# Attention weights made in layer 1, weight loads on GpSimd's queue, and the first two diffusions made among the projections of layer 2

## The chip, the cores and the metric

The kernel runs on one core of one Trainium2 chip. The metric is device time in microseconds (us) of one execution, lower is better. Times are medians of several executions; a profile is one further execution with the hardware profiler on.

## The reference, cut to what matters

Four graph layers run one after another on 4096 nodes with 256 features each, every one followed by a residual sum and a layernorm. Layer 0 is a masked attention over the adjacency matrix, layer 1 a dense product with it, layer 2 two steps of graph diffusion and top-p attention, layer 3 a mean over neighbours. The change lies in layer 1's first instructions and in layer 2:

```python
def layer1(x, adj, weight, bias):
    support = x @ weight
    return (diagonal(adj) + adj) @ support + bias

def layer2(X, S, W1, W2, W3, U1, U2, ln_g, ln_b):
    R = S + eye(N); R = R / R.sum(-1)
    Z, Xf, Xa = 0, X, X
    for n in range(2):
        q = Xa @ W1.T @ W2.T            # attention weights W1, W2, W3
        k = Xa @ W3.T
        probs = softmax(q @ k.T)
        A = top_p(probs, 0.9)           # keep the nucleus of each row, renormalise
        Xf = R @ Xf                     # diffusion
        Xa = A @ Xa                     # attention
        Z = Z + Xf @ U1[n].T + Xa @ U2[n].T   # projections
    h = X + Z
    return layernorm(h) * ln_g + ln_b

x = layernorm(x + layer1(x, adj, ...))
x = layernorm(x + layer2(x, adj, ...))
```

## The kernel before, in words

Rows are handled in 32 blocks of 128. X (the features, float32, all 32 blocks) and XD (a product's right-hand side, split into a high and a low part so that one 512-wide matmul does both) stay on the chip.

**Who decides the order.** Outside the parts under `manual_schedule` the framework orders each engine's instructions by its own estimate of when each is ready, so an instruction may stand far from its place in the source. On the chip each engine takes its own list strictly in order. A DMA is issued by an engine's queue (SP, ACT or POOL) at its place in that engine's list; if it must wait (for a buffer's last reader, say), everything behind it on that engine waits too.

**Layer 1.** `layer1` first transposes X in groups of four blocks (L108, copies L109), multiplies with w1 (L743) and splits the result into XD (L126, L127). Then, block by block, it multiplies the adjacency with XD (L764, 32 matmuls of 512 columns to a block), adds, normalises (L769 to L96) and writes the block to memory (L773, POOL's queue). Tiles `xT1[0]` and `xT1[1]` take the transposes in turn.

**Layer 2, its start.** `weights(0)` loads U1 and U2 of step 0 into `wt` (two DMAs, L1512) and ln_b into `affine` (L1513), on ACT's queue. Before that, in the source, W1, W3 and W2 are loaded into part of `es[0]` (L802, L803, ACT's queue too), W1 is transposed (L806, copied by L807), multiplied with W2 (L810), and the product and W3 are copied into `wkq` (L811, L812).

**keys.** For each of 8 groups of four blocks: transpose X (L891), copy to SBUF (L892; in step 0 the transposes of blocks 16 to 31 stay in `es[1]`), multiply with `wkq` (L896), copy keys and queries (L898, L899, L901, L902), transpose the keys (L905, L907), write the queries to memory (L910); moments of the keys (L913). Then the moments are worked into a small matrix (L914 to L932), and the centred keys go to `kT` (L924, L925, L926).

**scores, spreads, nucleus.** `scores(b)` multiplies a block's queries with all keys (L968) and takes the exponential (L970) into `es[b % 3]`. `spreads` makes a width for each row (L941, L945 to L955). `guessed` estimates a cut from it on ACT (L977, L1021), with a full pass on DVE for the first two blocks (L1055). `nucleus` finds the exact cut on DVE (L1122, L1126, small operations) and masks the row (L1176).

**project.** `project(step, b)` multiplies two blocks with `wt` (four L1453). In step 0, for blocks under 16, X is transposed anew (L1444, copied by L1447); for 16 and over `es[1]` is read. ACT writes XD's high part (L1457) and the part for Z (L1458, sent to memory by L1460), DVE the low part (L1459); POOL adds `affine` to X (L1462) and writes that (L1463). In step 1 ACT writes X and a summand (L1466, L1468) and POOL adds it to what was loaded (L1465, L1469, L1470). The loop takes the pairs b + 16 modulo 32 in the order b = 0, 2, ... 30. So `scores(1)`, which overwrites `es[1]`, stands after the eighth pair.

**Then** `weights(1)` loads `wt` and `affine` for step 1, `diffusion` multiplies blocks 0 and 1 of the adjacency with XD (L179; the pieces, four 128x128 tiles each, are loaded by SP, L176, three buffers), `diffused` and `keep` finish them (L1377, L1379, L1380, L1389), and the hand-ordered loop over blocks starts. In it each block has eight parts: four transposes of the masked row (L1325, copied by L1327) and four matmuls with X (L1334), with scores and the diffusion of a later block between them.

In step 1 the last such loads are of layer 3's weights (`w3` into `wt`, L1572, ACT's queue).

Of the kernel before, what the change touches and what calls it, by code (L numbers as in the profile page):

```python
# [9 lines left out]
F32 = mybir.dt.float32  # L10
# [13 lines left out]
P = 128  # L24
# [26 lines left out]
def row_broadcast(v, n):  # L51

    return bass.AP(tensor=v.tensor, offset=v.offset, ap=[[0, P], [1, n]])


class Net:
# [76 lines left out]
    def open_split(self):  # L133

        pool = self.ctx.enter_context(self.tc.tile_pool(name="split", bufs=1))
        self.XD = pool.tile([P, self.NB, 2, self.D], F32R, name="XD")

    def out_space(self):

# [583 lines left out]
        self.xT1 = [pool.tile([P, 2, 4 * P], F32, name=f"xT{i}") for i in range(2)]  # L723

    def add_w1(self):
        pool = self.pool1
        self.weight1, self.bias1 = self.load_w(pool, self.w1, "w1"), self.load_row(pool, self.b1, "bias1")

    def layer1(self):
        nc, tc, NB, D, X = self.nc, self.tc, self.NB, self.D, self.X  # L730
        with self.ctx1 as ctx:
            pool, w1, bias, dg = self.pool1, self.weight1, self.bias1, self.diagr
            work = ctx.enter_context(tc.tile_pool(name="l1w", bufs=2))
            psum = ctx.enter_context(tc.tile_pool(name="l1ps", bufs=2, space=PSUM))
            XD = self.XD
            for g in range(NB // 4):
                xT = self.transposed(psum, work, X[:, 4 * g:4 * g + 4, :], "xT", out=self.xT1[g % 2])
                if 1 <= g <= 4:
                    self.layernorm(work, self.later[g - 1], self.later[g - 1])
                for q in range(4):  # L740
                    ps = psum.tile([P, 512], F32, name="ps_sup")
                    for c in range(2):
                        nc.tensor.matmul(ps[:, :D], xT[:, c, q * P:(q + 1) * P], w1[:, c, :],  # L743
                                         start=(c == 0), stop=(c == 1))
                    self.split(XD[:, 4 * g + q], ps[:, :D])
            pd = psum.tile([P, 512], F32, name="ps_sup")
            for jc in range(NB):
                nc.tensor.matmul(pd, dg[:, jc:jc + 1].to_broadcast([P, P]), XD[:, jc].rearrange("p s d -> p (s d)"),
                                 start=(jc == 0), stop=(jc == NB - 1))
            row = pool.tile([P, D], F32, name="row1")  # L750
            nc.vector.tensor_add(row, pd[:, :D], bias)
            nc.vector.tensor_add(row, row, pd[:, D:])

            nas = []
            ahead = self.adj_pieces(work, nas, 0)
            for b in range(NB):
                ps = psum.tile([P, 512], F32, name="ps_adj")
                now, ahead = ahead, None
                for g, a in enumerate(now):

                    self.keep(work, a, b, g)
                    for k in range(8):
                        jc = g * 8 + k
                        nc.tensor.matmul(ps, a[:, k, :], XD[:, jc].rearrange("p s d -> p (s d)"),  # L764
                                         start=(jc == 0), stop=(jc == NB - 1))
                if b + 1 < NB:
                    ahead = self.adj_pieces(work, nas, b + 1)
                xb = X[:, b:b + 1, :]
                nc.vector.tensor_add(xb[:, 0], xb[:, 0], ps[:, :D])  # L769
                nc.vector.tensor_add(xb[:, 0], xb[:, 0], ps[:, D:])  # L770
                nc.vector.tensor_add(xb[:, 0], xb[:, 0], row)
                self.layernorm(work, xb, xb)
                nc.gpsimd.dma_start(self.xd[b, :, 0, :], xb[:, 0])  # L773


    def layer2(self):
        nc, tc, NB, D, X, N = self.nc, self.tc, self.NB, self.D, self.X, self.N
        A = 64
        HALF = N // 2
        with ExitStack() as ctx:  # L780
            self.ctx3 = ExitStack()
            rows2 = self.ctx3.enter_context(tc.tile_pool(name="l2", bufs=1))
            pool = ctx.enter_context(tc.tile_pool(name="l2s", bufs=1, side="right"))
            work = ctx.enter_context(tc.tile_pool(name="l2w", bufs=2, side="right"))
            psum = self.psum2 = self.ctx3.enter_context(tc.tile_pool(name="l2ps", bufs=2, space=PSUM))
# [5 lines left out]


            wt = pool.tile([P, 2, 2, D], F32, name="wt")
            wkq = pool.tile([P, 2, 2, A], F32, name="wkq")

            es = [rows2.tile([P, 4096], F32, name=f"e{i}") for i in range(3)]
            pre = es[0]
            aw1, aw3 = (pre[:, i * 128:(i + 1) * 128].rearrange("p (c m) -> p c m", c=2) for i in range(2))
            aw2 = pre[:A, 256:256 + A]
            w1 = pre[:A, 320:576].rearrange("p (c m) -> p c m", c=2)  # L800
            for t, w in ((aw1, self.aw1t), (aw3, self.aw3t)):
                nc.scalar.dma_start(t, w.rearrange("(c p) m -> p c m", p=P))  # L802
            nc.scalar.dma_start(aw2, self.aw2t)  # L803
            for c in range(2):
                pt = psum.tile([P, 512], F32, name="ps_tp")
                nc.tensor.transpose(pt[:A, :P], aw1[:, c, :], self.ident)  # L806
                nc.scalar.copy(w1[:, c, :], pt[:A, :P])  # L807
            for c in range(2):
                pt = psum.tile([P, 512], F32, name="ps_tp")
                nc.tensor.matmul(pt[:, :A], w1[:, c, :], aw2, start=True, stop=True)  # L810
                nc.vector.tensor_copy(wkq[:, c, 1, :], pt[:, :A])  # L811
                nc.vector.tensor_copy(wkq[:, c, 0, :], aw3[:, c, :])  # L812
            affine = pool.tile([P, D], F32, name="affine")
            rdeg = pool.tile([P, NB], F32, name="rdeg")
            nc.vector.tensor_scalar_add(rdeg, self.deg, 1.0)
# [41 lines left out]
            XD = self.XD  # L857
# [9 lines left out]
            def keys(step, src):  # L867
# [50 lines left out]
                nc.tensor.matmul(pc[:, :2 * A + 1], id2.rearrange("p s m -> p (s m)"), mom1, start=True, stop=True)  # L918
                nc.vector.tensor_copy(mom, pc[:, :2 * A + 1])

                for c in range(N // 1024):
                    cols = slice(c * 1024, (c + 1) * 1024)
                    kc = qs[:A, cols]
                    nc.vector.tensor_scalar(kc, kc, mom[:A, 2 * A:], None, op0=ALU.subtract)  # L924
                    nc.scalar.copy(kT[:A, cols], kc)  # L925
                    nc.vector.tensor_sub(kT[A:, cols], kc, kT[:A, cols].bitcast(F32))  # L926
# [418 lines left out]
            def diffusion(step, b):  # L1345


                pr = ps1.tile([P, 512], F32, name="ps_r")
                yield from self.adj_product(work, pr, b, lambda jc: XD[:, jc])
                return pr  # L1350
# [56 lines left out]
            def whole(steps):  # L1407

                while True:
                    try:  # L1410
                        next(steps)
                    except StopIteration as end:
                        return end.value
# [94 lines left out]
            def weights(step):  # L1508

                ut = (self.u1t, self.u2t)[step]  # L1510
                for i in range(2):
                    nc.scalar.dma_start(wt[:, :, i], ut[1 - i].rearrange("(c p) m -> p c m", p=P))  # L1512
                nc.scalar.dma_start(affine, row_broadcast((self.ln_b, self.ln_g)[step], D))  # L1513

            def piece(step, b, g, a=None):

# [8 lines left out]
            def times(ps, a, g, first=False, ks=range(4)):  # L1525

                for k in ks:
                    jc = 4 * g + k
                    nc.tensor.matmul(ps, a[:, k, :], XD[:, jc].rearrange("p s d -> p (s d)"),  # L1529
                                     start=(first and k == 0), stop=(jc == NB - 1))  # L1530

            def early(step, todo, banks, made):

# [12 lines left out]
            for step in range(2):  # L1546
# [8 lines left out]
                if step == 1:  # L1555
                    whole(scores(1, queries(1)))
                    guess = drained(guessed(step, 1))

                for b in range(0, NB, 2):
                    if b == 16 and step == 0:  # L1560
                        whole(scores(1, queries(1)))
                        guess = drained(guessed(step, 1))
                    if edge:
                        v = result(edge)
                        if v is not None:
                            rs[0], edge = v, None
                    project(step, (b + 16) % NB)
                if step == 0:
                    weights(1)
                else:  # L1570
                    for k in range(2):
                        nc.scalar.dma_start(wt[:, :, k], self.w3[k * D:(k + 1) * D].rearrange("(c p) m -> p c m", p=P))  # L1572

                if step == 0:
                    xb = base(step, 0)
                    pr = whole(diffusion(step, 0))
                    whole(diffused(step, 0, pr, xb))
                    whole(keep(step, 0, xb))
                    pr = whole(diffusion(step, 1))
                aTs = [turn(es[0], g) for g in range(2)]  # L1580
                q = queries(2)
                if step == 0:
# [350 lines left out]
```

## Time and profile before

| | us |
|---|---|
| median of 3 executions | 4052.07 |
| lowest, highest | 4050.99, 4052.44 |
| the profiled execution, its own time | 4052.79 |
| its span in the trace | 4051.1 |

The 1.7 us between the profiled execution's time and its span lie around the traced instructions. PE is the matmul engine, PEld its weight loads, DVE the vector engine, ACT the scalar engine, POOL GpSimd, SP the engine that only issues DMAs. A line of the timeline gives the start in us, the duration, engine, source line, operation, written and read tile, shapes, and the count; in brackets the engine's idle time ahead of it and what ended it. In the windows each engine's busy time is followed by its number of instructions, then come the granted TensorE clock (1.00 is full), the DMA engines' busy share, and GB/s.

### The profile page before, as it was taken

How to read it: one execution, taken by the hardware profiler on the slowest of the kernel's cores; microseconds unless marked ns; L12 is line 12 of the kernel's file. 1: busy time of each engine (PE TensorE's matmuls, PEld its weight loads, DVE VectorE, ACT ScalarE, POOL GpSimd, SP SyncE). 2: the span in 40 equal slices, each digit the busy share in tenths (PEclk: the TensorE clock that was granted, in tenths of full speed). 3: DMA queues.
4: the chain of work that ended last, by engine and by line, in shares of the span. 5: the costliest groups of instructions: out<-in, count | busy, mean ns of one | idle time of the engine just before them, and what ended most of it. 6: DMA issues, size and time to landing. Idle time of an engine off the chain costs nothing. (4 is left out here: it accounts for less than half of the span.)

```text
span 4051.1 us, 68763 instructions
## 1 busy us (share of the span) xinstructions
PE 3914.2 (97%) x25081; PEld 3388.4 (84%) x25081; DVE 2994.8 (74%) x6643; ACT 2755.4 (68%) x5127; POOL 1076.8 (27%) x1322
## 2 busy tenths in 40 slices
PE   8999999999999999799999999999999999999899
PEld 7899999999999788468888888864888888888687
DVE  7643228999999444548787887847899999999364
ACT  5543339999998322358888888835888888888132
POOL 0111110111333122301111111113455555555211
PEclk9999999999999999899999999999999999999999
DMA  4765547334221596433233323363333333335541
GB/s 137 230 208 177 179 151 214 96 103 125 70 87 51 222 379 270 121 107 97 95 99 98 103 92 102 105 227 98 105 116 106 103 113 111 103 114 189 185 159 47
DMA packets 322442, 556.42 MB, mean 137 GB/s; under 512 B 72134, under 2 KB 148550, under 8 KB 317990
## 3 DMA queue, kind: packets, MB, share of 16 engines
q1 hardware_dynamic: 239920, 395.13, 30.1%
q0 software_dynamic: 27664, 84.44, 6.2%
q10 hardware_dynamic: 54502, 72.27, 5.2%
q8 instruction: 203, 3.33, 0.3%
q14 instruction: 153, 1.25, 0.1%
HBM read 385.78 MB, written 165.94 MB: 136 GB/s over the span
## 5 line engine op out<-in xcount | busy, mean ns | idle before, releaser
L1334 PE MATMUL ps_a<-X,aT 128*128 128x256 f32 x4096 | 970.5, 380 | 1.3 <-ACT h L1475 1.1
L1334 PEld LDWEIGHTS ps_a<-X,aT 128*128 128x128 f32 x4096 | 776.0, 190 | 125.5 <-issue 3.3
L319 PE MATMUL acc<-gm,gt 128*128 128x198 bf16 x8192 | 706.4, 249 | 23.0 <-DMA gm<-gmd 6.7
L319 PEld LDWEIGHTS <-gt 128*128 128x128 fp8e4 x8192 | 703.1, 98 | 26.3 <-issue 9.3
L266 ACT ACTIVATE sg<-lpb,nlc 128x1024 fp8e4<-128x1024 f32 x636 | 667.2, 1135 | 61.3 <-DVE gt L268 38.6
L179 PE MATMUL ps_r<-XD,adj_piece 128*128 128x512 f32 x1952 | 548.1, 416 | 5.3 <-DMA adj_piece<-adjs 5.2
L537 PE MATMUL pz<-src,ar 128*128 128x264 f32 x4096 | 511.3, 288 | 14.2 <-DVE ar L527 12.2
L537 PEld LDWEIGHTS pz<-src,ar 128*128 128x128 f32 x4096 | 507.7, 190 | 17.7 <-DVE ar L527 11.8
L1061 ACT ACTIVATE ja<-e,nc 128x2048 uint8<-128x2048 f32 x240 | 480.9, 2004 | 2.0
L1327 ACT COPY aT<-ps_tp 128x512 f32<-128x512 f32 x512 | 295.9, 578 | 228.3 <-PE ps_tp L1325 226.4
L179 PEld LDWEIGHTS ps_r<-XD,adj_piece 128*128 128x128 f32 x1952 | 346.1, 190 | 78.9 <-issue 13.4
L530 ACT ACTIVATE nb<-a 128x512 uint8<-128x512 f32 x256 | 156.5, 630 | 288.6 <-DMA a<-in_adjt_dram 279.7
L1126 DVE MAX8 cand<-v 128x8 f32<-128x256 f32 x1024 | 347.1, 411 | 4.4
L1176 DVE SCALAR_TENSOR_TENSOR e<-e,edge 128x512 f32<-128x512 f32 x512 | 347.2, 750 | 2.2
L1325 PE MATMUL ps_tp<-ident,e 128*128 128x128 f32 x2048 | 308.2, 273 | 0.0
L1122 DVE SCALAR_TENSOR_TENSOR v<-e,hi 128x2048 f32<-128x2048 f32 x128 | 301.4, 2355 | 2.4
L1325 PEld LDWEIGHTS ps_tp<-ident,e 128*128 128x128 f32 x2048 | 257.1, 142 | 50.9 <-issue 0.5
L968 PE MATMUL ps_logit<-kT,q 128*128 128x512 f32 x1024 | 278.0, 414 | 12.1 <-DVE kT L926 6.6
L260 DVE TENSOR_SCALAR sg<-lpb,nlc 128x1024 fp8e4<-128x1024 f32 x384 | 285.1, 778 | 5.9 <-DVEq L357 3.9
L970 ACT ACTIVATE e<-ps_logit 128x1024 f32<-128x1024 f32 x256 | 259.8, 1025 | 29.9 <-PE ps_logit L968 28.8
L527 DVE CAST ar<-a 128x1024 fp32r<-128x1024 f32 x128 | 88.6, 693 | 232.9 <-PE pz L537 231.9
L764 PE MATMUL ps_adj<-XD,adj_piece 128*128 128x512 f32 x1024 | 243.5, 398 | 0.0
(383 smaller groups left out, 5497.0 us busy)
## 6 DMA issues: line engine op xcount, KB each, us to landing
adj_piece<-adjs SPq DMA_DIRECT2D x552, 256.0 KB
a<-in_adjt_dram SPq DMA_DIRECT2D x256, 256.0 KB
adjs<-adj_piece SPq DMA_DIRECT2D x96, 512.0 KB
na<-nad SPq DMA_DIRECT2D x64, 512.0 KB
nad<-nb POOLq DMA_DIRECT2D x128, 128.0 KB, 3.4
lpb<-lpd POOLq DMA_DIRECT2D x32, 512.0 KB, 4.0
na<-nad ACTq DMA_DIRECT2D x16, 1024.0 KB
gmd<-gb ACTq DMA_DIRECT2D x64, 198.0 KB
```

The costliest lines, as they stand in the source:

```text
L179: nc.tensor.matmul(ps, a[:, k, :], rhs(jc).rearrange("p s d -> p (s d)"), start=(jc == 0), stop=(jc == self.NB - 1))
L260: nc.vector.tensor_scalar(sg[:, k, :], lpb, nlc[:, 4 * g + k, h:h + 1], 2.0 ** -5, op0=ALU.is_ge, op1=ALU.mult, saturate=False)
L266: nc.scalar.activation(sg[:, k, :], lpb, AF.Sign, scale=-1.0, bias=nlc[:, 4 * g + k, h:h + 1], saturate=False)
L319: nc.tensor.matmul(acc[:, q, :6 * C1], gt[:, k, q * P:(q + 1) * P], gm0[:, k, :] if head0 else gm[:, jc, hh, :], start=(jc == 0 and q % 2 ...
L537: nc.tensor.matmul(pz[q][:, t, :W], ar[:, q, k, :], src[:, jc, t, s], start=(jc == 0 and s == 0), stop=(jc == NB - 1 and s == 1))
L1061: nc.scalar.activation(ja, e[:, s * HALF:(s + 1) * HALF], f, bias=nc1, accum_out=fs[:, i + s:i + s + 1])
L1122: nc.vector.scalar_tensor_tensor(v, ec, hi, ec, op0=ALU.is_lt, op1=ALU.mult, accum_out=sb[:, s:s + 1])
L1126: nc.vector.max(cand[:, 8 * j:8 * j + 8], v[:, k * 256:(k + 1) * 256])
L1176: nc.vector.scalar_tensor_tensor(ec, ec, edge[:, j:j + 1], ec, op0=ALU.is_ge, op1=ALU.mult)
L1325: nc.tensor.transpose(pt[:, k * P:(k + 1) * P], e[:, jc * P:(jc + 1) * P], self.ident)
L1327: nc.scalar.copy(aT, pt)
L1334: nc.tensor.matmul(pa[:, :D], aT[:, k * P:(k + 1) * P], X[:, jc, :], start=(jc == 0), stop=(jc == NB - 1))
```

## The change

1. The attention weights are loaded in layer 0, on POOL's queue, into `xT1[1]`, and `wkq` is made at the start of `layer1`. `wkq` moves to a pool that outlives layer 1.
2. The loads of `wt` and `affine` go from ACT's queue to POOL's: in step 0 before the keys, after the projections, and layer 3's weights after step 1's projections.
3. `project(step, 16)` is made inside `keys`, before the centred keys, in both steps; the loop skips it.
4. In step 0 the diffusions of blocks 0 and 1 are no longer made after the projections: from the pair b = 16 on, each turn of the loop adds four matmuls of each (`partly`), with the pieces in the order 4, 5, 6, 7, 0, 1, 2, 3. They have the PSUM tiles ps_a and ps_r.

```diff
+        self.wkq = pool.tile([P, 2, 2, 64], F32, name="wkq")      # open_split
...
     def add_w1(self):
         self.weight1, self.bias1 = ...
+        aw1, aw3, aw2, _ = self.attention_parts()
+        for t, w in ((aw1, self.aw1t), (aw3, self.aw3t)):
+            nc.gpsimd.dma_start(t, w.rearrange("(c p) m -> p c m", p=P))
+        nc.gpsimd.dma_start(aw2, self.aw2t)
+
+    def attention_parts(self):
+        A, t = 64, self.xT1[1]
+        halves = [t[:, 0, i * P:(i + 1) * P].rearrange("p (c m) -> p c m", c=2) for i in range(2)]
+        return [*halves, t[:A, 0, 2 * P:2 * P + A], t[:A, 1, :2 * P].rearrange("p (c m) -> p c m", c=2)]
+
+    def attention_weights(self, psum):
+        nc, A = self.nc, 64
+        aw1, aw3, aw2, w1 = self.attention_parts()
+        for c in range(2):
+            pt = psum.tile([P, 512], F32, name="ps_sup")
+            nc.tensor.transpose(pt[:A, :P], aw1[:, c, :], self.ident)
+            nc.scalar.copy(w1[:, c, :], pt[:A, :P])
+        for c in range(2):
+            pt = psum.tile([P, 512], F32, name="ps_sup")
+            nc.tensor.matmul(pt[:, :A], w1[:, c, :], aw2, start=True, stop=True)
+            nc.vector.tensor_copy(self.wkq[:, c, 1, :], pt[:, :A])
+            nc.vector.tensor_copy(self.wkq[:, c, 0, :], aw3[:, c, :])
...
             XD = self.XD
+            self.attention_weights(psum)                          # layer1
             for g in range(NB // 4):
...
-            (the same loads, on ACT's queue, transposes, matmuls and copies in layer2, in es[0] and ps_tp)
...
+                project(step, 16)                                 # keys, after the moments
                 for c in range(N // 1024):
...
                 for i in range(2):                                # weights
-                    nc.scalar.dma_start(wt[:, :, i], ut[1 - i].rearrange("(c p) m -> p c m", p=P))
-                nc.scalar.dma_start(affine, row_broadcast((self.ln_b, self.ln_g)[step], D))
+                    nc.gpsimd.dma_start(wt[:, :, i], ut[1 - i].rearrange("(c p) m -> p c m", p=P))
+                nc.gpsimd.dma_start(affine, row_broadcast((self.ln_b, self.ln_g)[step], D))
...
+            def partly(ps, b, g):
+                a = piece(0, b, g)
+                for k in range(4):
+                    nc.tensor.matmul(ps, a[:, k, :], XD[:, 4 * g + k].rearrange("p s d -> p (s d)"),
+                                     start=(g == 4 and k == 0), stop=(g == 3 and k == 3))
...
+                if step == 0:
+                    firsts = [ps1.tile([P, 512], F32, name=name) for name in ("ps_a", "ps_r")]
                 for b in range(0, NB, 2):
...
-                    project(step, (b + 16) % NB)
+                    if b:
+                        project(step, (b + 16) % NB)
+                    if b >= 16 and step == 0:
+                        for row in range(2):
+                            partly(firsts[row], row, (b // 2 - 4) % 8)
                 if step == 0:
                     weights(1)
                 else:
                     for k in range(2):
-                        nc.scalar.dma_start(wt[:, :, k], self.w3[...])
+                        nc.gpsimd.dma_start(wt[:, :, k], self.w3[...])
                 if step == 0:
                     xb = base(step, 0)
-                    pr = whole(diffusion(step, 0))
-                    whole(diffused(step, 0, pr, xb))
+                    whole(diffused(step, 0, firsts[0], xb))
                     whole(keep(step, 0, xb))
-                    pr = whole(diffusion(step, 1))
+                    pr = firsts[1]
```

In the changed program the framework's lists differ only near these places. PE has the same number of matmuls as before. The new lines get their names here: L745 to L752 make the attention weights, L1523 and L1524 are `weights`' loads, L1547 is `partly`'s matmul; all other lines are named by their number before the change.

More of the change, by code (lines that the diff above doesn't have):

```diff
@@ L725, in add_w1 @@
     def add_w1(self):
-        pool = self.pool1
+        nc, pool = self.nc, self.pool1
         self.weight1, self.bias1 = self.load_w(pool, self.w1, "w1"), self.load_row(pool, self.b1, "bias1")
+        aw1, aw3, aw2, _ = self.attention_parts()
[18 more added lines that the diff above has]
+            nc.vector.tensor_copy(self.wkq[:, c, 0, :], aw3[:, c, :])
     def layer1(self):
@@ L793, in layer2 @@
             wt = pool.tile([P, 2, 2, D], F32, name="wt")
-            wkq = pool.tile([P, 2, 2, A], F32, name="wkq")
+            wkq = self.wkq
             es = [rows2.tile([P, 4096], F32, name=f"e{i}") for i in range(3)]
[L797 to L812, printed above, removed]
             affine = pool.tile([P, D], F32, name="affine")
@@ L1571, in layer2 @@
                     for k in range(2):
-                        nc.scalar.dma_start(wt[:, :, k], self.w3[k * D:(k + 1) * D].rearrange("(c p) m -> p c m", p=P))
+                        nc.gpsimd.dma_start(wt[:, :, k], self.w3[k * D:(k + 1) * D].rearrange("(c p) m -> p c m", p=P))
                 if step == 0:
                     xb = base(step, 0)
-                    pr = whole(diffusion(step, 0))
-                    whole(diffused(step, 0, pr, xb))
+                    whole(diffused(step, 0, firsts[0], xb))
                     whole(keep(step, 0, xb))
-                    pr = whole(diffusion(step, 1))
+                    pr = firsts[1]
                 aTs = [turn(es[0], g) for g in range(2)]
```

## The prediction

> **What bounds the kernel now.** I read the page's busy times first:
>
> ```profile
> PE 3914.2 (97%) x25081; PEld 3388.4 (84%) x25081; DVE 2994.8 (74%) x6643; ACT 2755.4 (68%) x5127; POOL 1076.8 (27%) x1322
> ```
>
> PE is busy 97% of the span. A block loop behind the change has no gap (80.00 of 80 us from 1820 to 1900), so time won on PE ahead of that loop should stay won. So I looked for idle PE where the diff works, in windows from the end of layer 1 to the first loop:
>
> ```profile
> core 0: us, PE busy (x) PEld busy (x) DVE busy (x) ACT busy (x) POOL busy (x), PEclk, DMA share, GB/s
> 1620.00:1632.00 12.00, 5.44 (x28) 4.32 (x29) 3.95 (x33) 2.39 (x4) 3.21 (x5) 0.79 0.48 145
> 1632.00:1669.00 37.00, 29.58 (x177) 18.46 (x175) 19.60 (x33) 17.41 (x25) 14.63 (x15) 0.92 0.69 176
> 1669.00:1695.00 26.00, 25.82 (x109) 16.70 (x110) 14.19 (x26) 11.75 (x34) 12.77 (x14) 0.89 0.20 79
> 1695.00:1706.00 11.00, 1.06 (x9) 0.82 (x7) 4.33 (x1) 4.66 (x16) 3.70 (x4) 0.66 0.23 86
> 1706.00:1764.00 58.00, 54.74 (x149) 26.48 (x148) 35.19 (x81) 25.67 (x63) 0.60 (x2) 0.98 0.18 63
> 1764.00:1792.00 28.00, 22.60 (x88) 16.52 (x86) 2.52 (x5) 4.39 (x10) 1.09 (x2) 0.88 0.56 185
> ```
>
> Length minus PE busy, added up, is 32.8 us of idle PE in 172 us, and the clock is below 1.00 after each pause. PE's waits name the pauses:
>
> ```profile
> PE ps_tp L1444 <- ACT aT L1447: 11.4, 2, 9.9
> PE ps_tp L806 <- DMA adj_piece<-adjs: 4.8, 1, 4.8
> PE ps_r L179 <- DMA adj_piece<-adjs: 3.9, 4, 1.8
> PE ps_logit L968 <- DVE kT L926: 3.6, 1, 3.6
> ```
>
> The longest is no slow copy. ACT's timeline shows what it stood behind:
>
> ```profile
> 1690.61 0.39 ACT L977 ACTIVATE z<-z,cs,t 128x1 f32<-128x1 f32 x1 [0.16 <-ACT z L977]
> 1700.14 0.35 ACTq L1513 DMA_DIRECT2D affine<-in_ln_g_dram  x1
> 1700.59 0.39 ACT L977 ACTIVATE z<-z,qsp,t 128x1 f32<-128x1 f32 x1 [9.59 <-POOL part L1462]
> ```
>
> The load of step 1's `affine` sits early in ACT's list and may not overwrite what POOL still adds. POOL makes one pair's add every 4.1 us and begins the last at 1698.86. So ACT stood 9.59 us; behind it stood the estimate (L977, L1021) that DVE's pass L1055 needs, and the copy L1447 that PE needs. At the other pause, layer 2's start, ACT's first copy L892 stands behind five weight loads. Those of L802 and L803 wait for layer 1's memory. The PE timeline shows where that leads:
>
> ```profile
> 1627.71 0.61 PE L806 MATMUL ps_tp<-ident,e 128*64 128x128 f32 x2 [4.82 <-DMA adj_piece<-adjs]
> ...
> 1631.25 3.13 PE L896 MATMUL ps_tp<-e,wkq 128*128 128x512 f32 x4
> ...
> 1705.50 1.11 PE L1444 MATMUL ps_tp<-ident,X 128*128 128x128 f32 x4 [9.94 <-ACT aT L1447]
> 1706.83 18.42 PE L1453 MATMUL ps_logit<-wt,e 128*128 128x512 f32 x40 [0.21 <-DVE XD L1459]
> ...
> 1771.49 3.78 PE L179 MATMUL ps_r<-XD,adj_piece 128*128 128x512 f32 x8 [1.83 <-DMA adj_piece<-adjs]
> ```
>
> **What the Trainium skill says.** "DMA: Bandwidth & Descriptors", in the anatomy of one DMA on the gpsimd path: the DMA engines wait on no semaphore; the issuing engine's sequencer does, before dispatch. ACT's 9.59 us agree. The same page, on issuing engines not being separate DMA queues: all share 16 engines, so moving a load wins only the issuer's time and waits. The windows cannot test that. "TensorE: Matmul & The Clock Gate", Part 1: half clock after an idle window of some 3.4 us. The trace agrees in kind, and at shorter gaps too: after 1.83 us idle, eight L179 took 3.78 us, later ones 2.14. "SBUF — State Buffer", on DVE blocking DMA: DVE can hold up GpSimd's writing of descriptors. No row here tests it; it is what could make POOL's loads dearer than their 0.72 to 0.78 us (L1463).
>
> **The change, part by part.** I replayed the changed lists with the durations of before.
>
> (1) Attention weights in layer 1. Ahead of L743 stand 2 transposes, 2 ACT copies, 2 matmuls and 4 small DVE copies: 0.6 + 0.5 + 0.6 us of PE and copies (L806, L807, L810), partly beside L108, whose transposes ran 1.06 us and whose tile copies follow. L743 begins at about 1331.05 for 1329.76: **+1.3 us** (0 if the wait for DVE's L325 covers it; +3 if DVE, where 0.85 us of copies stand in front, delays the tiles). The three loads in layer 0 cost nothing: POOL there is some 10% busy and the data is needed far later.
>
> (2) Layer 2's start. L806 to L812 and ACT's five issues go. POOL now issues `wt` (2 x 0.75 us) about where the last block's normalisation runs there, so L96 ends at 1624.15 for 1623.36. ACT's first L892 then runs 1624.2 to 1625.2, and L896 begins at 1625.25 for 1631.25: **-6.0 us** (-6.6 without POOL's delay; -3.5 if it still stands until the transfer that ended L806's wait, 1627.7).
>
> (3) A projection beside the keys. A group of keys takes 3.79 us, paced by L896, L898, L899/L901 in turn; PE is idle about 0.9 us in it. Eight L1453 records at 0.44 us (20 in 8.85), 3.5 us, go into that, and the list puts the first `partly` matmuls there too. I take +0.8 to the moments' end: L918 begins at about 1658.5 for 1663.74 (**-5.2 so far**), with 3.5 us of later work done (0 to +3.5 on the delay).
>
> (4) The `affine` load stands on POOL behind the adds that it waits for. Behind it on POOL are the guesses of the first nucleus (L1143, L1157), not needed before about 1710, and the adds end near 1699.5: no cost. ACT runs on; L1055 can begin near 1686.7 for 1701.67. The projections that went on at 1706.83 go on at 1692.1: **-14.7 so far**, with 8 of the 64 `partly` matmuls done.
>
> (5) The remainder, from 1692.1 to the place reached at 1792.10 before. On PE: 96 L1453 at 0.44, 42.2 us; 24 L968, 6.1; 16 L1444, 2.4; 56 `partly` at 0.235 (128 L764 records ran at about that without a pause), 13.2; L1325 1.0; L1334 1.7: 66.6 us. Idle left I estimate at 4: a wait for scores(2)'s L970 (1.57 before), one for `XD` from DVE, the first pieces. Before, the same stretch held 85.3 us, with 5 idle among the diffusions and their cold clock (8 in 3.78 against 2.14), which go because a late piece now has projections beside it. So 1762.7 for 1792.1: **-29.4 so far** (-33 with no idle; -18 if 11 more idle comes back). What is late next: DVE, whose L1459 for the first new pair stands behind L1055, ending 9.3 us after scores(1), while PE has 10.6 us of other work; and SP, which must bring 13 pieces on demand through three buffers. POOL has the two `wt` loads for step 1 (1.5 us) ahead of L1380, on which ACT's L1389 waits; they end before L1379 can.
>
> (6) Step 1 (2680 to 2840, where the waits list 12.8 us of idle PE). The projection in the keys delays the moments by some 2.4 us; later one projection (3.5) and one POOL pair (4.1) fewer lie ahead of the last one. L968 waits for ACT's L1468 (1.3 and 1.1) shrink; `w3` on POOL stands before the last L1469 but is needed only from 2902. **-1.7 us** (-3.5 to +2).
>
> Sum: +1.3 - 29.4 - 1.7 = -29.8, against the profiled execution's 4052.79, which is 0.7 above the median. That is 4022.3 on the median's scale; as a hand replay misses small waits, I add 2 and forecast **4024**.
>
> **The rivals.** (A) A new wait takes a part. In (2) L896 may stand until 1627.7 (2.5 less); in (5) DVE's order or SP's pieces may leave 11 us more. 2.5 to 13.5 less gives 4026 to 4038, with a slow keys stretch and step 1's upper end (2.7 + 3.7) up to 4044. For it: each pair is a chain of PE, ACT, DVE and SP, and PE takes its list in order. Against: DVE has 35 of 58 us busy there.
>
> (B) No change: POOL gives it back. If the `wt` loads in front of L89 are held up by DVE, layer 2 starts later by what each costs over 0.75 us, and L1462's chain, at 4.1 us to a pair, shifts with it. About 15 us of held-up issue on both and 13 us of other waits leave 4050. Against: L1463 never took over 1.1 us there.
>
> (C) Slower. In (5) PE stands in its list before each four `partly` matmuls until the piece is there, where before a piece could only delay other diffusions. Then 4 of 16 pieces were late, 3.9 us in all, the longest 1.83 us and 1.7 more by the cold clock. If each of the 13 pieces cost that 3.5 us, 45 us are lost against 29.8 won: 4052.1 + 16 = 4068. It decides from 2.3 us a piece. For it: DMA from 1764 to 1792 was at 185 GB/s, and a wait queues L1453 behind it. Against: spread over 60 us, 13 pieces of 256 KB are only 57 GB/s, where 63 GB/s left the DMA engines at 0.18.
>
> That the change does little of what it says belongs to (B): loads moved to another queue whose waits still end last.
>
> **How the numbers follow.** 0.2% is 8.1 us, about what a measurement can tell from no change. Forecast within -33 to -24 us: 0.58; rival A: 0.25; B, within 8 us either way: 0.07; C and other losses: 0.10. A's and the forecast's cases are faster; of A I give 0.01 to no change. So faster 0.82, same 0.08, slower 0.10. Range: from the open end of (2), (5) and (6) together (0.6 + 3.6 + 1.8 below 4022, so 4016) up to A's 4044.
>
> **What would show it right or wrong.** Right: no idle on ACT of over 3 us around the `affine` load, which is on POOL's queue; first L896 about 4 to 6 us after the last L764's end; between the moments and the end of the diffusions PE idle below 10 us; the loop's first blocks some 28 us earlier. (1): the first L743 about 1.3 us later. (3): keys at about 4 us to a group while the projection is in it. Wrong: waits of L1547 for pieces that add up to over 10 us, or of L1444 or L1453 for DVE behind L1055; POOL's L89 or L1462 late behind L1523; a loop that gives the start back.

## The result, and the profile after

| | before | changed |
|---|---|---|
| median, us (6 executions each) | 4053.44 | 4034.73 |
| lowest, highest | 4050.99, 4063.0 | 4030.8, 4042.04 |
| span of the profiled execution | 4051.1 | 4034.4 |

The ratio is 0.9949, 95% interval 0.9935 to 0.9963: 20.7 us faster (15 to 26), where the two medians differ by 18.7. Single executions of one kernel lie 8 to 21 us apart and before's median drifts between sets of runs, which ran on two chips (4053 to 4060), so below kernels are compared by their ratio to before in the same set, and stages by the trace.

Profile lines of the changed kernel carry its own line numbers: layer 1's L743 is L769 there and L764 is L790; L891, L892, L896, L907 are L901, L902, L906, L917; from L926 on 11 is added (L968 is L979, L1447 is L1458, L1453 is L1464, L1529 is L1540); L179 is L180. The text keeps before's names. First the page's span and busy times:

```profile
span 4034.4 us, 68767 instructions
...
PE 3912.9 (97%) x25081; PEld 3383.5 (84%) x25081; DVE 2994.1 (74%) x6643; ACT 2757.1 (68%) x5127; POOL 1088.5 (27%) x1333
```

PE's busy time is 1.3 us less than before, the span 16.7 us: idle went, not work. The windows from the end of layer 1 to the first blocks of the loop (columns as before):

```profile
core 0: us, PE busy (x) PEld busy (x) DVE busy (x) ACT busy (x) POOL busy (x), PEclk, DMA share, GB/s
1624.00:1636.00 12.00, 6.94 (x27) 4.57 (x28) 3.85 (x30) 2.39 (x3) 5.11 (x8) 0.72 0.41 132
1636.00:1673.00 37.00, 32.32 (x187) 19.59 (x186) 21.28 (x34) 18.34 (x27) 14.64 (x16) 0.96 0.72 185
1673.00:1700.00 27.00, 26.52 (x117) 17.03 (x116) 17.99 (x28) 16.32 (x49) 13.34 (x14) 0.93 0.24 83
1700.00:1758.00 58.00, 57.57 (x182) 31.60 (x183) 34.27 (x80) 24.95 (x61) 5.06 (x7) 1.00 0.37 119
1758.00:1769.00 11.00, 9.99 (x40) 6.50 (x40) 2.79 (x5) 4.42 (x10) 2.23 (x3) 1.00 0.68 205
```

Length minus PE busy gives 11.7 us of idle PE in 145 us, for 32.8 in 172. The window of 11 us with PE at 1.06 is gone. What is left lies mostly at the start: 5.1 us in the first window, the clock at 0.72, and 4.7 in the second. PE's waits from 1600 to 1800:

```profile
PE ps_logit L979 <- DVE kT L937: 4.2, 2, 3.8
PE ps_tp L906 <- ACT e L902: 4.1, 1, 4.1
PE ps_logit L901 <- DVE X L796: 1.1, 1, 1.1
PE ps_logit L979 <- ACT e L981: 0.9, 1, 0.9
...
PE ps_a L1547 <- DVE XD L1470: 0.2, 1, 0.2
```

The 11.4 us at L1444 and the 3.9 us for pieces are no longer in the list; no L1547 waited for a piece. PE's timeline has the marks to lay beside before's 1631.25, 1706.83 and 1792.10:

```profile
1631.00 3.78 PE L906 MATMUL ps_tp<-e,wkq 128*128 128x512 f32 x4 [4.07 <-ACT e L902]
...
1700.72 14.00 PE L1464 MATMUL ps_logit<-wt,e 128*128 128x512 f32 x32
...
1768.79 2.20 PE L979 MATMUL ps_logit<-kT,q 128*128 128x512 f32 x8 [0.95 <-ACT e L981]
```

I cut both programs into stages between PE instructions that both have, named by before's lines. Layers 0 and 3 are left out, as they differ by up to some 6 us between executions, edited or not. The table gives two profiled executions of each kernel (the second ones are among the experiments).

| stage, us | before | changed | forecast | found |
|---|---|---|---|---|
| last L319 to first L743 | 3.50, 3.50 | 4.85, 4.87 | +1.3 | +1.4 |
| first L743 to first L748 | 54.75, 59.37 | 58.32, 58.76 | 0 | +0.8 (a third wait); the rest within the spread |
| first L891 to first L896 | 10.30, 10.40 | 6.01, 6.00 | -6.0 | -4.3 |
| first L896 to first L918 | 32.49, 33.16 | 35.50, 34.61 | +0.8 | +2.2 |
| first L918 to the loop (65th L1334) | 154.89, 155.42 | 128.79, 129.06 | -24.2 | -26.2 |
| the loop (to the 501st L968) | 797.25, 797.25 | 797.25, 797.25 | 0 | 0 |
| boundary of the steps (501st L968 to 49th L1529) | 56.01, 56.48 | 59.84, 55.88 | 0 | open |
| step 1 (65th L891 to 2301st L1334) | 246.54, 248.53 | 247.15, 248.31 | -1.7 | +0.2 here, +1.8 over 14 runs |

The loop takes the same time to 0.01 us in every run: what is won ahead of it arrives behind it.

### The profile page after: what moved, and what is told of

Read it like the earlier page. It is cut to its first block, busy times and chain, and to the rows that moved or that the text cites. A ratio compares the mean times of both kernels' runs of the same rounds, so it can differ in the third digit from the quotient of the medians.

```text
span 4034.4 us, 68767 instructions
## 1 busy us (share of the span) xinstructions
PE 3912.9 (97%) x25081; PEld 3383.5 (84%) x25081; DVE 2994.1 (74%) x6643; ACT 2757.1 (68%) x5127; POOL 1088.5 (27%) x1333
## 5 line engine op out<-in xcount | busy, mean ns | idle before, releaser
L180 PE MATMUL ps_r<-XD,adj_piece 128*128 128x512 f32 x1888 | 528.4, 414 | 0.3 <-DMA adj_piece<-adjs 0.3
L180 PEld LDWEIGHTS ps_r<-XD,adj_piece 128*128 128x128 f32 x1888 | 332.9, 189 | 69.3 <-issue 12.9
L979 PE MATMUL ps_logit<-kT,q 128*128 128x512 f32 x1024 | 276.8, 412 | 12.4 <-DVE kT L937 8.0
L790 PE MATMUL ps_adj<-XD,adj_piece 128*128 128x512 f32 x1024 | 244.9, 399 | 0.0
```

The lines of the kernel that those rows point to most:

```text
L180: nc.tensor.matmul(ps, a[:, k, :], rhs(jc).rearrange("p s d -> p (s d)"), start=(jc == 0), stop=(jc == self.NB - 1))
```

## The experiments

My theory after the result: three things win and add (the load that held ACT, the diffusions among the projections, the attention weights out of layer 2's start), and part is given back where GpSimd now issues loads. The rival: the waits move, and what is given back is chance of the write-backs and piece loads.

### One edit alone, or one left out

**Attention weights alone** (e1_weights_alone): the kernel before with the first edit only.

> The kernel before with the first edit alone: attention weights made at layer 1's start. Theory (the parts add, and layer 1 pays for the weights): layer 2's first L896 follows the first L891 after 6 us or less instead of 10.3, so -4 to -6 us there; the last-issued L743 wait and the start of layer 1 cost what the changed kernel's trace shows, +4.9; the ACT wait of 9.6 us at the affine load and the waits among the diffusions stay. Sum 0 to -2 us, and layer 1's end (last L764) about 4 to 5 us later than before's. Rival (layer 1's 4.9 us are a matter of when its write-backs to memory land, whatever the program): layer 1's end within 1.5 us of before's, sum -4 to -6 us.

4052.69 us, ratio 0.9996 (0.9987 to 1.0005). First L896 comes 3.63 us after first L891 (10.30), so that stage wins 6.7. The first L743 is 1.26 us later relative to layer 0's end, and first L743 to first L748 took 59.72. As expected, the start's gain is hardly seen at the end. If layer 1 had to pay only the 1.26, 5.4 us would be left, and the interval ends at 5.3; what else layer 1 pays is taken up below.

**The queue alone** (e2_queue_alone): the kernel before with the second edit only.

```diff
-                    nc.scalar.dma_start(wt[:, :, i], ...)
-                nc.scalar.dma_start(affine, ...)
+                    nc.gpsimd.dma_start(wt[:, :, i], ...)
+                nc.gpsimd.dma_start(affine, ...)
```

> The kernel before with the second edit alone: the loads of wt, affine and layer 3's weights on GpSimd's queue. Theory: the 9.9 us wait of PE at L1444 goes, the projections resume 10 to 15 us earlier, and most of it reaches the end; layer 2's start gives 2 to 3 us back, because GpSimd's L88 stands behind the first wt load. Sum -8 to -12 us. Rival (the wait moves: DVE's pass L1055 or SP's pieces hold PE next): the projections resume earlier, but the diffusions' waits grow by as much, sum -4 us or less in size. Layer 1's end must be within 1.5 us of before's if it is edit one that delays it.

4048.63 us, ratio 0.9989 (0.9982 to 0.9995), some 4.5 us: less than I expected, and near the rival's size. But the rival's mechanism fails: L918 to the loop is 144.49 (before 154.89), so the wait is gone there and stays gone, and PE's waits for pieces among the diffusions are 3.5 us in all, for 3.9 before. The loss is elsewhere: first L891 to first L896 is 13.87 (10.30), the keys 34.09 (32.49), and the boundary 60.06 (56.01) in this execution. The edit wins 10.4 in one place and loses 5.2 at layer 2's start.

**Diffusions after the projections** (e3_not_among): the changed kernel without its fourth edit.

> The changed kernel without its fourth edit: the first two diffusions after the projections again. Theory: PE again waits for pieces and runs slow after the pauses, as before's 64 L179 did (5 us idle, some 6 of slow clock), and the idle at the moments and among the last projections is not filled: 8 to 12 us slower than the changed kernel, about 4043 to 4046. Rival (the pieces came late only because SP issues them late, and with the affine wait gone they come in time): within 3 us of the changed kernel.

4045.63 us, ratio 0.9976 (0.9969 to 0.9984) against 0.9949: about 11 us slower than the changed kernel. L918 to the loop is 142.96 for 128.79. PE's waits in this kernel show what comes back:

```profile
PE ps_r L180 <- DMA adj_piece<-adjs: 4.1, 4, 1.7
...
PE ps_tp L1455 <- ACT aT L1458: 2.6, 2, 1.6
```

The pieces are late again although the `affine` wait is gone, so the rival (late only because of that wait) fails. Spread over the projections, the same loads are in time. The changed kernel's list has neither of these two lines.

**No projection beside the keys** (e4_not_beside): the changed kernel without its third edit.

> The changed kernel without its third edit: no projection inside the keys, in either step. Theory (the keys are a chain, and the eight matmuls stretch it by nearly their own time): step 0's moments come 2 to 3 us earlier, 3.5 us of projection come back later; step 1 gains 0 to 2 us: within 2 us of the changed kernel. Rival (the projection fills idle PE in the keys at no cost, as I forecast with +0.8 of 3.5 in step 0 and -1.7 in step 1): 4 to 5 us slower than the changed kernel.

4032.73 us, ratio 0.9949 (0.9934 to 0.9964), the same as the changed kernel. The stages show parts that nearly cancel: in step 0 first L918 to the loop is 133.32 for 128.79 (the edit wins 4.5), the keys 33.83 for 35.50 and 34.61 (it costs 0.8 to 1.7); in step 1 the keys, from their first L891 to L918, are 43.27 for 45.21.

### Which of the loads wins

**Step 1's `affine` alone** (f3_affine_alone): the kernel before with one load on GpSimd's queue.

```diff
-                nc.scalar.dma_start(affine, ...)
+                (nc.scalar, nc.gpsimd)[step].dma_start(affine, ...)
```

> The kernel before with one load moved: only step 1's affine goes to GpSimd's queue. Theory (the wait of ACT behind this one load is all that the second edit wins): the 9.9 us wait of PE at L1444 is gone, the stretch from the moments (first L918) to the first blocks of the loop is 9 to 11 us shorter as with the whole second edit (10.4), and nothing is given back at layer 2's start: 7 to 11 us faster than before. Rival (the wt loads of step 1 on ACT hold it next, or the boundary between the steps gives it back as with the whole edit, 4.7): 2 to 6 us faster.

4048.13 us, ratio 0.9974 (0.9967 to 0.9982), 10.6 us faster. L918 to the loop is 143.03, 11.9 less than before. In PE's waits, what was 11.4 us at L1444 is

```profile
PE ps_tp L1444 <- ACT aT L1447: 2.5, 2, 1.5
```

One load of the eight that the second edit moves makes its whole gain, and more than all eight together (0.9989 in another set, on the other chip; the two intervals touch).

**Step 0's loads back on ACT** (f1_first_on_act): the changed kernel, but

```diff
-                    nc.gpsimd.dma_start(wt[:, :, i], ...)
-                nc.gpsimd.dma_start(affine, ...)
+                    (nc.scalar, nc.gpsimd)[step].dma_start(wt[:, :, i], ...)
+                (nc.scalar, nc.gpsimd)[step].dma_start(affine, ...)
```

> The changed kernel with step 0's three loads (wt twice, affine) on ACT's queue as before; step 1's and layer 3's stay on GpSimd's. Theory (GpSimd's L88 and L89 of the last block stand behind and between the first wt loads, and that delays L96 and so ACT's L892): first L896 about 9 us after the first L891 ended layer 1's wait less 4 to 5, that is 3.5 to 5 us after it, where the changed kernel has 6.0 and the kernel with the weights alone 3.7; 2 to 3.5 us faster in all. Rival (ACT's L892 is then late behind these loads, or the keys lose their start again): within 1 us of the changed kernel. The projections resume as early as in the changed kernel in both.

4035.66 us, ratio 0.9935 (0.9917 to 0.9954). By time it can't be told from the changed kernel, as the intervals overlap; by stage it can: first L891 to first L918 is 36.58 us for the changed kernel's 41.51 and 40.61. To see why, lay two timelines side by side. The changed kernel, POOL and DVE at layer 2's start:

```profile
1624.88 0.42 DVE L797 TENSOR_TENSOR X<-X,row 128x256 f32<-128x256 f32 x1
...
1627.02 0.73 POOL L1523 DMA_DIRECT2D wt<-in_u1t_dram  x1 [6.14 <-PE ps_logit L901]
1627.78 0.23 POOL L88 TENSOR_SCALAR ln_var<-ln_mv 128x1 f32<-128x1 f32 x1
1627.95 0.77 POOL L1523 DMA_DIRECT2D wt<-in_u1t_dram  x1
1628.74 0.58 POOL L89 TENSOR_TENSOR ln_rstd<-ln_var,power 128x1 f32<-128x1 f32 x1
...
1629.36 0.41 DVE L96 TENSOR_SCALAR X<-X,ln_mv,ln_rstd 128x256 f32<-128x256 f32 x1 [2.97 <-POOL ln_rstd L89]
```

And with step 0's loads on ACT: ACT and POOL, and PE after them:

```profile
1630.67 0.91 ACTq L1523 DMA_DIRECT2D wt<-in_u1t_dram  x2
```

```profile
1631.42 0.22 POOL L88 TENSOR_SCALAR ln_var<-ln_mv 128x1 f32<-128x1 f32 x1 [5.21 <-DVE ln_mv L86]
1631.72 0.57 POOL L89 TENSOR_TENSOR ln_rstd<-ln_var,power 128x1 f32<-128x1 f32 x1
```

```profile
1633.96 1.98 PE L906 MATMUL ps_tp<-e,wkq 128*128 128x512 f32 x4 [1.69 <-ACT e L902]
```

On GpSimd the first `wt` load is issued at 1627.02, 1.72 us after DVE's last use of layer 1's memory has ended (L797, before's L771, at 1625.30). L88 could run at 1626, when its input is there, but it stands behind this load, and L89 behind the second one; DVE's L96 waits 2.97 us. With the loads on ACT, they issue 0.04 us after that instruction ends, L88 runs when its input is there, and L96's wait is 0.74. The difference is 2.4 us to the first L896.

A second price comes with it. After 4.07 us of idle PE the first four L896 take 3.78 us, at a granted clock of 0.50 (1631 to 1635); with the loads on ACT they take 1.98 after 1.69 us, at 1.00. From the first group's L896 to the second's it is 6.26 us in the changed kernel (5.40 in its second execution), here 3.78. But before's start was slow too (4.92 and 5.59), so against before this price is only some 0.6 us. The rest of the keys' extra length is the projection: the two groups of keys that hold it take 4.6 to 4.8 and 4.6 us for 3.8, some 1.6 us together, in all eight executions that have it.

**Only step 1's `affine` on GpSimd** (h1_only_affine): the changed kernel with all other loads back on ACT.

> The changed kernel with only step 1's affine load on GpSimd's queue; wt of both steps, step 0's affine and layer 3's weights on ACT's. Theory (of the second edit only this one load wins anything, the others only cost): first L891 to first L918 36 to 37 us, where the changed kernel has 41.5; L918 to the loop's first blocks 128 to 130 us as there; the boundary between the steps (block 15's first L968 after #500 to the 49th L1529) back at 55.9 to 56.5, where the kernels with step 1's wt on GpSimd had 57.7 to 60.8. Sum 6 to 9 us faster than the changed kernel. Rival (the boundary's 2 to 4 us follow from how the pieces' loads fall, not from that queue): boundary 57.7 or more, sum 3 to 5 us faster.

4030.41 us, ratio 0.9931 (0.9918 to 0.9944) where the changed kernel, in the same set, had 0.9949 (0.9937 to 0.9961). First L891 to first L918 is 37.38, a little over what I expected (ACT's issue of step 0's `affine` took 1.73 us for 0.48 in the kernel above, and ACT's first L892 stands behind it), the boundary 56.02, as expected. The two intervals overlap, so by time the gain over the changed kernel is likely, not shown.

### Chance, and what is the change's own

**Weights in the middle of layer 1** (f2_weights_late): the changed kernel with

```diff
-            self.attention_weights(psum)          # ahead of the first transposes
...
+                if b == 4:
+                    (the three loads, on GpSimd's queue)
+                if b == 8:
+                    self.attention_weights(psum)
```

> The changed kernel with the attention weights made in the middle of layer 1 (loads at block 4, transposes and products at block 8) instead of at its start, so that the instructions of layer 1's start stand as before. Theory (at its start the weights shift the order there, PE waits a third time for L127, and ACT's L203 waits 4.5 to 5.9 us for write-backs, together 3 to 6 us): layer 1 from the last L319 to the last L764 takes 293 + 1 to 2 us, where the four kernels with weights at its start take 296.4 to 299.4 and the two without take 293.2 and 294.5. Sum 2 to 4 us faster than the changed kernel. Rival (how the write-backs fall is chance): 296 us or more again.

4037.4 us, ratio 0.994 (0.9922 to 0.9959). First L743 is back at 3.50 after the last L319; L748 to the last L764 takes 236.04 for 235.01, the weights' own 1.0 us of PE. But layer 1 in all is 297.01, where I expected 294 to 295 and the rival 296 or more: no clear gain. The same kernel splits the 2.4 us at layer 2's start. Its `wt` loads stand on GpSimd too, yet the first is issued 0.59 us after its last reader on DVE (1625.08 to 1625.67), and the trace names no wait (this kernel's L1525 is before's L1512):

```profile
1625.67 0.73 POOL L1525 DMA_DIRECT2D wt<-in_u1t_dram  x1 [5.01 <-issue]
```

L96 waits 1.84 us, and first L896 comes 4.87 us after first L891: 1.2 more than with the loads on ACT, 1.1 less than in the changed kernel. There, and in the four other executions with the weights at layer 1's start and step 0's `wt` on GpSimd, the load is issued 1.7 us after DVE, and the trace names the end of PE's L891, 0.1 us earlier. So about half of the loss is the two issues ahead of L88 and L89, and half is, by the trace, a wait of the load for PE; why the load waits for PE in those kernels is not shown.

**The kernel before again** (f4_before_again).

> The kernel before, unchanged, profiled once more. It shows how far stages that the edits do not touch differ between two executions: layer 0 (so far by 3.4 us between kernels), layer 1, the last diffusions of step 0 with the first of step 1 (so far -0.4 to +4.7 us against before), layer 3. If the boundary between the steps differs by 2 us or more from the first profile, what the changed kernel lost there (3.6) is not shown to be its own.

4065.23 us in one execution. First L743 to first L748 took 59.37 for 54.75, with no edit at all. ACT's wait that I had put down to the changed order is there too:

```profile
ACT adj_piece L203 <- DMA adjs<-adj_piece: 5.0, 1, 5.0
```

PE's waits from 1318 to 1410, in this kernel and in the changed one, still differ:

```profile
PE ps_sup L743 <- DVE XD L127: 7.3, 2, 3.8
```

```profile
PE ps_sup L769 <- DVE XD L127: 7.8, 3, 3.7
```

The third wait, of 0.7 to 0.9 us, is there in each of the eight executions with the weights at the start and in none of the other six. So of layer 1's 4.9 us in the first profile some 2 are the change's own (1.3 ahead of L743, 0.8 behind it); the rest comes without it as well. Over all runs the stage from L743 to L748 averages 57.9 with the weights at the start (8 runs) and 56.8 without (6), with overlapping values.

**The changed kernel again** (h4_after_again).

> The changed kernel again, for its own spread: layer 1's start (last L319 to first L748) 61.5 to 64.5 us, first L891 to first L896 6.0, the boundary between the steps 57.7 to 60.8, if these belong to the change; layer 1's start or the boundary at before's 58.3 to 59.5 or 55.9 to 56.5, if they were chance.

4038.09 us, ratio 0.9949 (0.9937 to 0.9961). Layer 1's start and the 6.0 us repeat, but the boundary is 55.88, like before's. I had come to think that step 1's `wt` on GpSimd makes the boundary longer; this execution refutes that it always does. The six kernels without that load there lie between 55.9 and 56.6, the eight with it between 55.9 and 60.8. Six of those eight are 57.7 or more, which makes the load suspect; but in the changed kernel `wt` is loaded at 1762 and layer 3's weights at 2815, the boundary runs from 2592 to 2652, and no moved load is issued in it. What the longer ones have in most cases is a longer wait of L1529 for a piece (2.9 to 3.8 us for 1.6 to 2.0). Whether the load makes them likelier is not settled.

**The projection beside the keys in step 0 alone** (h3_beside_once): the changed kernel with

```diff
-                project(step, 16)
+                if step == 0:
+                    project(step, 16)
...
-                    if b:
+                    if b or step == 1:
```

> The changed kernel with the projection beside the keys in step 0 alone. Theory (in step 1 it lengthens the keys by 2.3 us and wins back about 1): step 1's keys 42.9 to 43.3 us for 45.2, step 1 from its first L891 to L1334 #2300 about 1.5 us shorter than the changed kernel's 247.2; the rest as the changed kernel. Rival (it pays in step 1, as I forecast with -1.7): that stretch 1 us or more longer.

4036.66 us, ratio 0.9945 (0.9931 to 0.9959), not told from the changed kernel. Step 1's keys are 42.87 us, the whole stretch 245.43. Over all runs that stretch averages 246.3 without the projection (8 runs, 245.1 to 248.5) and 248.1 with it (6 runs, 247.2 to 248.6): so on the average it costs 1.8 us there. The ranges overlap (e4_not_beside took 247.90 without it), so the size is rough; a gain is nowhere to be seen.

**All together** (h2_best): weights at blocks 4 and 8 of layer 1, only step 1's `affine` on GpSimd, the projection beside the keys in step 0 alone, diffusions among the projections.

> What the experiments point to: attention weights in the middle of layer 1, only step 1's affine on GpSimd's queue, a projection beside the keys in step 0 alone, diffusions among the projections. Theory: the last kernel's gain plus 1.5 us in step 1 and about 1 us in layer 1: 8 to 12 us faster than the changed kernel, .9915 to .993 of before. Rival (the parts don't add where loads saturate the DMA engines): not more than 4 us faster than the changed kernel.

4027.64 us, ratio 0.9925 (0.9912 to 0.9938): some 10 us faster than the changed kernel in the same set, the fastest kernel here. The intervals of the two just touch, and it can't be told from h1_only_affine; it is better than the changed kernel by the stages (first L891 to first L918 39.11 for 41.51 and 40.61, step 1 245.61) and likely so by time.

## Why the prediction was right or wrong

The direction, the place and the mechanism were right: idle PE between layer 1 and the loop, most of it from one load that held ACT. The parts were forecast to win 29.8 us, 27.8 after an allowance of 2 for small waits; 20.7 (15 to 26) were measured. That lies where the forecast had put rival (A). Of what (A) named, the waits for DVE's order and for pieces did not come; a late first L896, slow keys and a loss in step 1 did. Parts (2), (3) and (6) fell short and layer 1 had one more wait, while (5) won 2 us more than forecast; that the errors partly cancel is luck.

- **(1)** right as far as it went: +1.3 forecast, +1.1 to +1.5 in the eight runs with the weights at the start. It missed the third wait for L127, 0.8 us more. The rest of layer 1's loss in the first profile comes in the kernel before as well.
- **(2)** right in sign, mis-sized in one term. I priced GpSimd's `wt` loads at +0.8 on L96. Measured, L96 ends 2.4 us later relative to first L891: the first load is issued only at 1627.02, not when DVE is done with the memory, and L88 waits behind it. Without that delay (f2_weights_late) it is 1.2. Found -4.3 for -6.0; with the loads on ACT -6.7 (f1_first_on_act), at my lower bound, and -5.9 (h1_only_affine). First L896 comes 7.1 us after the last L764's end, for the 4 to 6 that I had named, and one of the signs of being wrong, POOL's L89 late behind L1523, came. Rival (B) had the place right, in that those loads stand in front of L89; its size was too large.
- **(3)** +0.8 forecast for the keys, +2.2 found. The two groups that hold the projection are 1.6 longer, at 4.6 us a group for my "about 4": the projection's 3.5 us of matmuls fit in less well than I took. The other 0.6 is the slower start after the pause of (2), within what before's two executions differ by (0.7).
- **(4)** right: the projections resume 34.2 us after first L918 (1666.50 to 1700.72) for 43.1, 8.9 less, where I had 9.5. One load alone shows it in f3_affine_alone.
- **(5)** right, a little better than forecast: from the resumption to the last scores 68.1 us (1700.72 to 1768.79) for my 70.6; I had left 4 us of idle, and PE's windows show 1.4 to the end of that stretch. Rivals (A) and (C) both needed waits for DVE or for pieces in it; the largest of either is 0.2 us (L1547 for DVE's L1459). e3_not_among shows that the diffusions' place is worth 14.2 of the 26.2 us, e4_not_beside that the projection beside the keys is worth 4.5, f3_affine_alone the load at 11.9 in before's own order. The three sum to 30.6: they overlap.
- **(6)** wrong in sign: -1.7 forecast, +1.8 over 14 runs. I expected L968's waits for L1468 (2.4 us) to shrink. PE's waits from 2680 to 2850, before and then changed, show that they grew, and the wait for the keys with them:

```profile
PE ps_logit L968 <- DVE kT L926: 3.1, 2, 2.6
...
PE ps_logit L968 <- ACT part L1468: 1.3, 1, 1.3
PE ps_logit L968 <- ACT dif L1468: 1.1, 1, 1.1
```

```profile
PE ps_logit L979 <- DVE kT L937: 3.8, 1, 3.8
PE ps_logit L979 <- ACT dif L1479: 3.1, 1, 3.1
```

In the second executions the waits for L1468 are 2.8 us for 2.0. The delay of the keys (2.3 us for my 2.4) was right; what was to be won back behind it was not.

With layer 1's third wait the stages add to +1.4 + 0.8 - 4.3 + 2.2 - 26.2 + 1.8 = -24.3, within the timed interval. The 3.6 us between it and the 20.7 may be the boundary's longer executions and layer 1's write-backs; that is not shown.

## What to carry to other kernels

When several loads move to another queue, price each by itself: what waits behind it on the old queue, and what will stand behind it on the new one. Here one load made the edit's gain, and the others, moved along with it, put 4 us back at a place where a short normalisation was the next thing that PE needed. A pause of PE can be paid twice, in the wait and in slow matmuls after it, and independent work whose inputs come late is best spread among work that is ready. Before a stage's loss is put down to a change, profile the kernel before a second time.

## What the runs showed of the hardware

The same `wt` load, behind the same last reader on DVE (L771), was issued 0.04 us after it on ACT (1630.63 to 1630.67, f1_first_on_act) and 0.59 us after it on GpSimd where the trace names no other wait (1625.08 to 1625.67 in f2_weights_late, 1623.83 to 1624.42 in e2_queue_alone). The 1.72 us of the changed kernel (1625.30 to 1627.02) are not a price of GpSimd's queue alone: the trace names PE's L891 there.

How slow PE is after a pause is not a function of the pause alone: after the same 4.07 us the first four L896 took 3.78 and 2.68 us in the two executions of the changed kernel; after 2.36 us they took 3.20 (h2_best, the granted clock 0.50 from 1632 to 1634), after 2.49 us 1.98 (h1_only_affine, 1.00 throughout).
